# A four-layer graph network on one core: later layers' preparation spread over the steps before they need it, with a new set of planner constants

## The chip, the cores and the metric

The kernel runs on one core of one Trainium2 chip. The metric is the device time of one execution in microseconds (us). A core has a matrix engine (TensorE, PE in the profile, with its weight loads as PEld), a vector engine (VectorE, DVE), a scalar engine (ScalarE, ACT), a general engine (GpSimd, POOL) and a queue that issues DMAs (SyncE, SP). Each works through its own queue in order; semaphores tie them together.

## The reference

There are 32 samples `x` of 512 nodes by 256 features, and one adjacency matrix `adj` of 512 by 512, the same for all samples. Four layers follow each other, each with a layer norm and a relu ahead and a residual behind. Layer 0 is masked multi-head attention with four heads of 64, layer 1 a pair of small graph attention nets with an MLP around them, layer 2 graph attention with four heads of 64, layer 3 the same with eight heads of 32 and a prior made of `adj`:

```python
h = jnp.maximum(_layernorm(x, axis=-1), 0.0)
x = x + _L0_gnn_ref(h, adj, wq, bq, wk, bk, wv, bv, wo, bo)
h = jnp.maximum(_layernorm(x, axis=-1), 0.0)
x = x + _L1_gnn_ref(h, adj, mlp1_w, mlp1_b, mlp2_w, mlp2_b, W_fc, a_fc, W_hand, a_hand)
h = jnp.maximum(_layernorm(x, axis=-1), 0.0)
x = x + _L2_gnn_ref(h, adj, W, a)
h = jnp.maximum(_layernorm(x, axis=-1), 0.0)
x = x + _L3_gnn_ref(h, adj, adj[None], W, a_src, a_dst, beta_tilde, W_out)
```

In layer 3 the attention score of each pair gets `softplus(beta_tilde) * log(prior + 1e-6)` added before a masked softmax. All arithmetic is float32.

## The kernel before

**Preparation.** A first part (lines 400 to 456) loads `adj`, the first sample and the weights of layer 0, transposes `adj`, and makes `mask0T`. What only the later layers need is built by `preparation` as a list of small functions, the pieces: three groups of weight loads (`first_loads`, `second_loads`, `third_loads`, all on SP's queue), `mask_t` (four slices of `mask1T`, VectorE), `output_bias` (the bias of layer 0's output with the value bias folded in: two matmuls and an addition), `fc` (eight) and `hand` (four), which reduce rows of `W_fc` and `W_hand` with the attention vectors of layer 1 on VectorE, `column_sums` (the bias of layer 1's second MLP), `project` (eight) and `scaled` (two), which do the same for layers 2 and 3, `softplus` (beta of layer 3, and the logarithm of the four slices of `mask3T`, on ScalarE), and `mask_3` (four: an exponential on ScalarE and a product with `mask1T` on VectorE).

**The plan.** The work of the 32 samples is not issued as it is written. A `Plan` records every operation as a `Step` (all of them show as L276 in the profile, the line that issues them) with an engine, an assumed duration, what it reads and what it writes. `order` then simulates the engines with these durations and builds one list: at each turn it takes, of all steps that are ready, the one that could start first, and of equals the one that is due first. A step's due time is

```python
step.due = s * self.period - step.tail - step.urgent
```

where `s` is the sample, `period` the constant PERIOD, `tail` the assumed length of the chain from this step to the sample's end, and `urgent` an entry of the table URGENT, looked up by the kind of tile that the step writes and its layer ("p3:3" is the attention weights of layer 3; a negative entry puts them off). STARTS, PACE and LAYERS give the earliest times at which the samples, and the layers in them, may be planned. Buffers are counted too: 62 blocks of 128 x 512 (`tag="block"`) and the 8 banks of PSUM; FILLED = 10 blocks are taken as occupied, by the preparation, until FILLED_TO. Up to four samples are in work at once, and four buffers hold `x`.

**The issue.** `issue` goes through this list and emits the instructions. The pieces of preparation are not in the plan; from step LATE = 30 on, one is emitted at every second step until none is left:

```python
for n, step in enumerate(self.order()):
    if late and n > LATE:
        assert step.layer == 0
        if n % 2:
            late.pop(0)()
    for attribute, op, args, kw in step.calls:
        getattr(getattr(self.nc, attribute), op)(*args, **kw)
```

In the trace the pieces stand under their own lines: L510 to L513 `output_bias`, L519 `column_sums`, L525 `fc`, L531 `hand`, L539 and L540 `project`, L543 and L544 `scaled`, L547 `mask_t`, L551 to L558 `softplus`, L562 and L563 `mask_3`.

**A sample's path.** In layer 0, scores `sc` (TensorE) become `p` (Exp on ScalarE, then times `mask0T` on VectorE), are summed into `total` on VectorE and multiplied with the values into `av`; two heads share a matmul by tiling TensorE's rows or columns. `normalise` sends the sums through DRAM and back as `rc`, `oT` is their product with the copied `av`, and `mm<-woT,oT` closes the layer. An accumulating DMA on GpSimd's queue (`x<-boa`) adds the output bias to `x`; it is the first `dma_start` of that engine in the plan. Layers 2 and 3 (`separable`) make `p3` from broadcast rows `R` in the same way, with `mask1T` and `mask3T`.

Of the kernel before, what the change touches and what calls it, by code (L numbers as in the profile page):

```python
# [22 lines left out]
NT = N // P  # L23
D = 256
KD = D // P
HID = 512
KH = HID // P
# [14 lines left out]

PERIOD = 134.0
STARTS, PACE = (0.0, 0.0, 82.0, 163.0), 113.0
LAYERS = (0.0, 48.0, 0.0, 189.0)

URGENT = {
    "pt:0": 166, "mm:0": 75, "sc:0": 126, "total:0": 49, "pt:1": 25, "mm:1": 40, "nd:1": 9, "p1:1": 126,  # L50
    "total:2": -404, "ue:2": -193, "mm:3": -135, "p3:3": -681, "av:3": -684, "total:3": -608,
}
BLOCKS, KEEP = 62, 2
KEEP_BANKS = 0

LATE = 30

FILLED, FILLED_TO = 10, 120.0
BANKS = ("mm", "av", "sm", "sc", "pt")


# [8 lines left out]
class Plan:  # L70
# [77 lines left out]
    def release(self, sample, layer):  # L148

        first = len(STARTS) - 1  # L150
        return (STARTS[sample] if sample < first else STARTS[first] + (sample - first) * PACE) + LAYERS[layer]

# [112 lines left out]

    def issue(self, tc, late):

        late = list(late)
        with tc.manual_schedule():
            for n, step in enumerate(self.order()):  # L270
                if late and n > LATE:
                    assert step.layer == 0
                    if n % 2:
                        late.pop(0)()
                for attribute, op, args, kw in step.calls:
                    getattr(getattr(self.nc, attribute), op)(*args, **kw)  # L276

# [68 lines left out]
def gnn_stack_kernel(ctx: ExitStack, tc: tile.TileContext, a: dict, out: bass.AP):  # L346
# [18 lines left out]
    def T(ap, rearr, **kw):  # L365
        return ap.rearrange(rearr, **kw)
# [44 lines left out]
    first = ctx.enter_context(tc.tile_pool(name="first", bufs=1))  # L411
# [7 lines left out]
    with prep_stack, tc.manual_schedule():  # L419

        adj = prep.tile([P, NT, N], I32, name="adj", bufs=1)
        av = T(a["adj"], "(t p) j -> p t j", p=P)
# [8 lines left out]
        for name in ("bq", "bk", "bv", "mlp1_b", "mlp2_b"):  # L431
            n = a[name].shape[0]
# [32 lines left out]
    def preparation(block, bank):  # L465

        todo = []
# [94 lines left out]
            nc.scalar.activation(mask3T[:, j, :], mask3T[:, j, :], AF.Exp, scale=beta)  # L562
            nc.vector.tensor_tensor(mask3T[:, j, :], mask3T[:, j, :], mask1T[:, j, :], op=ALU.mult)  # L563

        todo += [first_loads, second_loads, third_loads] + [partial(mask_t, j) for j in range(NT)] + [output_bias]
        todo += [partial(fc, k, c) for k in range(KH) for c in range(2)] + [column_sums]
        todo += [partial(hand, k, c) for k in range(KD) for c in range(2)]
        v2 = [a2[:, None, c * F2 : (c + 1) * F2].to_broadcast([P, H2, F2]) for c in range(2)]
        for w, h, f, vs, vd in ((w2, H2, F2, *v2), (w3, H3, F3, *(T(v, "p (h f) -> p h f", h=H3) for v in (s3, d3)))):
            for k in range(KD):  # L570
                todo += [partial(project, w, k, h, f, vs, w[:, :, :h]), partial(project, w, k, h, f, vd, w[:, :, 3 * h + D :])]
            todo.append(partial(scaled, w, h))
        return todo + [softplus] + [partial(mask_3, j) for j in range(NT)]

    def pipelined(stack):

# [2 lines left out]
        dram = stack.enter_context(tc.tile_pool(name="dram", bufs=6, space=bass.MemoryType.DRAM))  # L579
        q = Plan(nc, PERIOD)  # L580
        def block(name):

            return q.tile(big, [P, N], name, BLOCKS, keep=KEEP, tag="block")
# [433 lines left out]
        for i in range(B):  # L1017
# [9 lines left out]
        q.layer = 3  # L1027
        tests()
        late = preparation(
            lambda n: big.tile([P, N], F32, tag="block", name=n, bufs=BLOCKS),  # L1030
            lambda n: psum.tile([P, N], F32, tag="bank", name=n, bufs=8),
# [424 lines left out]
```

## Time and profile before

| what | us |
|---|---|
| median of 3 runs (3978.35 to 3980.23) | 3978.85 |
| the profiled execution | 3979.58 |
| its span, first to last instruction | 3977.5 |
| TensorE busy | 3888.6 |
| VectorE busy | 3341.5 |
| ScalarE busy | 2807.2 |
| GpSimd busy | 563.8 |

The span is the time that the profile covers; the execution's own time has about 2 us around it. Busy time of TensorE is modelled, since its matmuls are pipelined. A float32 matmul appears as two records: 512 columns take 0.43 us each from start to start. In timelines the number in brackets is the idle time of the engine before a row, with what ended it.

### The profile page before, as it was taken

How to read it: one execution, taken by the hardware profiler on the slowest of the kernel's cores; microseconds unless marked ns; L12 is line 12 of the kernel's file. 1: busy time of each engine (PE TensorE's matmuls, PEld its weight loads, DVE VectorE, ACT ScalarE, POOL GpSimd, SP SyncE). 2: the span in 40 equal slices, each digit the busy share in tenths (PEclk: the TensorE clock that was granted, in tenths of full speed). 3: DMA queues.
4: the chain of work that ended last, by engine and by line, in shares of the span. 5: the costliest groups of instructions: out<-in, count | busy, mean ns of one | idle time of the engine just before them, and what ended most of it. 6: DMA issues, size and time to landing. Idle time of an engine off the chain costs nothing.

```text
span 3977.5 us, 52568 instructions
## 1 busy us (share of the span) xinstructions
PE 3888.6 (98%) x17144; PEld 2146.2 (54%) x17144; DVE 3341.5 (84%) x7049; ACT 2807.2 (71%) x5968; POOL 563.8 (14%) x530
## 2 busy tenths in 40 slices
PE   7999999999999999999999999999999999999986
PEld 3655555565555555555555555555555555555542
DVE  6389988888988888988888988888988889888886
ACT  4467667776777766777766777666777767677665
POOL 0001111101111111111101111011111011111010
PEclk8999999999999999999999999999999999999998
DMA  3013333313233233333223333132333233333231
GB/s 92 17 49 76 75 84 83 80 55 89 59 89 91 62 74 73 72 89 83 65 65 81 73 88 86 51 89 57 83 92 77 58 76 75 84 83 77 64 74 51
DMA packets 217617, 292.58 MB, mean 74 GB/s; under 512 B 49915, under 2 KB 103422, under 8 KB 217334
## 3 DMA queue, kind: packets, MB, share of 16 engines
q0 software_dynamic: 68864, 111.18, 16.1%
q1 hardware_dynamic: 148196, 177.69, 14.3%
q8 instruction: 138, 2.26, 0.2%
q14 instruction: 145, 1.19, 0.1%
q10 hardware_dynamic: 274, 0.26, 0.0%
HBM read 158.79 MB, written 19.10 MB: 45 GB/s over the span
## 4 chain that ended last, share of the span: by engine, by line
PE 70%; DVE 17%; DMA 5%; ACT 4%; issue 2%; POOL 2%; SPq 1%; DVEq 0%; ACTq 0%; POOLq 0%
PE mm L276 33%; PE av L276 23%; PE sc L276 5%; PE pt L276 5%; DVE p L276 5%; DVE total L276 5%; DMA R<-rd 4%; PE sm L276 3%; POOL rs L276 2%; DVE o L276 1%; ACT p L276 1%; DVE x L276 1%; DVE ue L276 1%; DVE stats L276 1%; DVE y L276 1%
## 5 line engine op out<-in xcount | busy, mean ns | idle before, releaser
L276 ACT ACTIVATE p<-R,e 128x512 f32<-128x512 f32 x1536 | 987.7, 724 | 53.0 <-DMA R<-rd 52.9
L276 PE MATMUL av<-p,v 128*128 128x512 f32 (+1 forms) x2560 | 933.8, 598 | 13.0 <-ACT p L276 10.7
L276 DVE SCALAR_TENSOR_TENSOR p<-p,e,mask3T 128x512 f32<-128x512 f32 x1024 | 718.8, 749 | 16.9 <-ACT p L276 16.9
L276 POOL TENSOR_TENSOR rs<-ve,mhalf 128x4 f32<-128x4 f32 x128 | 206.5, 1613 | 2755.6 <-DVE ve L276 2202.6
L276 PEld LDWEIGHTS av<-p,v 128*128 128x128 f32 (+1 forms) x2560 | 347.6, 169 | 458.0 <-issue 367.3
L276 DVE TENSOR_TENSOR total<-total,p 128x512 f32<-128x512 f32 x872 | 573.2, 689 | 0.5
L276 PE MATMUL av<-p,vs 128*32 128x512 f32 (+1 forms) x3072 | 494.9, 597 | 5.3 <-DVE p L276 5.0
L276 PE MATMUL mm<-W_fc,o 128*128 128x256 f32 (+1 forms) x2048 | 469.0, 380 | 2.5 <-ACT o L276 2.3
L276 PEld LDWEIGHTS mm<-W_fc,o 128*128 128x128 f32 x2048 | 382.3, 190 | 86.5 <-issue 29.4
L276 POOL DMA_DIRECT2D p<-p x360 | 317.3, 1014 | 579.5 <-PE av L276 161.9
L276 DVE SCALAR_TENSOR_TENSOR p<-p,e,mask1T 128x512 f32<-128x512 f32 x512 | 347.9, 750 | 41.4 <-ACT p L276 40.7
L276 ACT ACTIVATE h<-x,ms,rs 128x256 f32<-128x256 f32 x512 | 282.8, 629 | 128.5 <-DVE ms L276 128.4
L276 DVE TENSOR_TENSOR p<-p,mask0T 128x512 f32<-128x512 f32 x512 | 329.3, 690 | 20.0 <-ACT p L276 20.0
L276 PEld LDWEIGHTS av<-p,vs 128*32 128x32 f32 (+1 forms) x3072 | 136.5, 118 | 334.8 <-issue 234.3
L276 DVE TENSOR_TENSOR total<-p,p 128x512 f32<-128x512 f32 x436 | 289.2, 688 | 0.0
L276 ACT ACTIVATE p<-sc 128x512 f32<-128x512 f32 x512 | 254.4, 684 | 6.1 <-PE sc L276 6.1
L276 PE MATMUL mm<-w,hT 128*128 128x272 f32 (+1 forms) x1024 | 254.0, 394 | 1.1 <-ACT hT L276 1.0
L276 PE MATMUL mm<-hT,mlp_w 128*128 128x512 f32 x512 | 237.3, 595 | 0.6 <-ACT hT L276 0.6
L276 PE MATMUL mm<-o,mlp_w 128*128 128x512 f32 x512 | 234.2, 595 | 0.3
L276 PE MATMUL sc<-qT,kT 64*128 64x512 f32 x1024 | 228.4, 596 | 0.0
L276 PEld LDWEIGHTS mm<-w,hT 128*128 128x128 f32 x1024 | 191.3, 192 | 61.5 <-issue 14.3
L276 ACT COPY v<-mm 128x512 f32<-128x512 f32 (+2 forms) x384 | 166.1, 470 | 43.7 <-PE mm L276 40.7
(182 smaller groups left out, 5321.1 us busy)
## 6 DMA issues: line engine op xcount, KB each, us to landing
R<-rd SPq DMA_DIRECT2D x384, 256.0 KB
p<-p POOLq DMA_DIRECT2D x360, 256.0 KB, 5.4
x<-in_x_dram SPq DMA_DIRECT2D x32, 512.0 KB
x<-boa POOLq DMA_DIRECT2D x32, 512.0 KB, 5.6
rc<-s SPq DMA_DIRECT2D x128, 128.0 KB
out_dram<-x SPq DMA_DIRECT2D x32, 512.0 KB
rc<-s SPq DMA_DIRECT2D x248, 64.0 KB
s<-sums SPq DMA_DIRECT2D x94, 8.0 KB
```

The lines of the kernel that those rows point to most:

```text
L276: getattr(getattr(self.nc, attribute), op)(*args, **kw)
```

## The change

Three things are changed. The constants of the plan (PERIOD, STARTS, PACE, LAYERS, URGENT, FILLED_TO) take other values. The list of pieces carries with each piece the layer that it has to precede: 0 for the loads and `output_bias`, 1 for `fc`, `column_sums`, `hand` and `mask_t`, 2 for `project`, `scaled`, `softplus` and `mask_3`. And `issue` distributes the pieces of each group evenly, by step number: those of group 0 between step 30 and the first accumulating DMA of GpSimd, those of group 1 from there to the first step of layer 1, those of group 2 from there to the first step of layer 2. `mask_t`, which came before `output_bias`, now comes after `hand`; else the order in the list is kept.

```diff
-PERIOD = 134.0
-STARTS, PACE = (0.0, 0.0, 82.0, 163.0), 113.0
-LAYERS = (0.0, 48.0, 0.0, 189.0)
+PERIOD = 179.0
+STARTS, PACE = (0.0, 0.0, 38.0, 159.0), 85.0
+LAYERS = (0.0, 4.0, 2.0, 98.0)
 
 URGENT = {
-    "pt:0": 166, "mm:0": 75, "sc:0": 126, "total:0": 49, "pt:1": 25, "mm:1": 40, "nd:1": 9, "p1:1": 126,
-    "total:2": -404, "ue:2": -193, "mm:3": -135, "p3:3": -681, "av:3": -684, "total:3": -608,
+    "pt:0": 192, "mm:0": 49, "total:0": 70, "av:0": 68, "mm:1": 25, "total:1": -78, "rs1:1": 42, "av:1": -7,
+    "p2:1": 104, "p3:2": -95, "total:2": -542, "ue:2": -396, "mv:3": -121, "mm:3": -158, "p3:3": -723,
+    "av:3": -527, "total:3": -695,
 }
...
-FILLED, FILLED_TO = 10, 120.0
+FILLED, FILLED_TO = 10, 190.0
...
-        late = list(late)
+        steps, at = self.order(), {}
+        begin = LATE
+        for layer in range(3):
+
+            pieces = [f for need, f in late if need == layer]
+            first = next(n for n, step in enumerate(steps) if step.layer > layer - 1 and n > begin) if layer else next(n for n, step in enumerate(steps) if step.calls[0][1] == "dma_start" and step.engine == "POOL")
+            for i, f in enumerate(pieces):
+                at.setdefault(begin + (first - begin) * i // len(pieces), []).append(f)
+            begin = first
         with tc.manual_schedule():
-            for n, step in enumerate(self.order()):
-                if late and n > LATE:
-                    assert step.layer == 0
-                    if n % 2:
-                        late.pop(0)()
+            for n, step in enumerate(steps):
+                for f in at.get(n, ()):
+                    f()
                 for attribute, op, args, kw in step.calls:
                     getattr(getattr(self.nc, attribute), op)(*args, **kw)
...
-        todo += [first_loads, second_loads, third_loads] + [partial(mask_t, j) for j in range(NT)] + [output_bias]
-        todo += [partial(fc, k, c) for k in range(KH) for c in range(2)] + [column_sums]
-        todo += [partial(hand, k, c) for k in range(KD) for c in range(2)]
+        todo += [(0, f) for f in (first_loads, second_loads, third_loads, output_bias)]
+        todo += [(1, partial(fc, k, c)) for k in range(KH) for c in range(2)]
+        todo += [(1, column_sums)] + [(1, partial(hand, k, c)) for k in range(KD) for c in range(2)]
+        todo += [(1, partial(mask_t, j)) for j in range(NT)]
...
-                todo += [partial(project, w, k, h, f, vs, w[:, :, :h]), partial(project, w, k, h, f, vd, w[:, :, 3 * h + D :])]
-            todo.append(partial(scaled, w, h))
-        return todo + [softplus] + [partial(mask_3, j) for j in range(NT)]
+                todo += [(2, partial(project, w, k, h, f, vec, dst)) for vec, dst in ((vs, w[:, :, :h]), (vd, w[:, :, 3 * h + D :]))]
+            todo.append((2, partial(scaled, w, h)))
+        return todo + [(2, softplus)] + [(2, partial(mask_3, j)) for j in range(NT)]
```

## The prediction

> **What bounds the kernel now.** I read the page first, then busy time by windows, then the timelines of TensorE and ScalarE where a window is not full, and last the end of the chain of waits.
>
> ```profile
> span 3977.5 us, 52568 instructions
> ...
> PE 3888.6 (98%) x17144; PEld 2146.2 (54%) x17144; DVE 3341.5 (84%) x7049; ACT 2807.2 (71%) x5968; POOL 563.8 (14%) x530
> ...
> PEclk8999999999999999999999999999999999999998
> ```
>
> TensorE is idle for 3977.5 - 3888.6 = 88.9 us in all. The windows say where: of the first 400 us it is busy 370.3 (idle 29.7), from 400 to 3800 it is busy 3384.8 of 3400 (idle 15.2), from 3800 to the end 133.6 of 177.5 (idle 43.9). So the whole change can win only at the start, at the end, or by making the packed middle itself denser.
>
> ```profile
> 40.00:60.00 20.00, 9.35 (x33) 3.26 (x30) 13.28 (x34) 13.55 (x25) 0.00 (x0) 0.66 0.00 0
> 60.00:80.00 20.00, 20.00 (x77) 9.04 (x76) 12.90 (x22) 8.27 (x15) 0.00 (x0) 1.00 0.01 2
> 80.00:100.00 20.00, 15.35 (x58) 7.89 (x58) 18.20 (x33) 6.25 (x13) 0.00 (x0) 0.83 0.08 27
> ...
> 643.60:883.90 240.30, 239.28 (x1057) 132.16 (x1056) 207.59 (x437) 173.84 (x373) 36.96 (x34) 1.00 0.32 76
> ...
> 3769.70:3977.40 207.70, 163.86 (x843) 83.29 (x841) 153.39 (x318) 121.09 (x258) 16.44 (x16) 0.90 0.25 68
> ```
>
> The columns are the stretch, its length, busy time (and count) of TensorE, its weight loads, VectorE, ScalarE, GpSimd, then TensorE's granted clock, DMA share and GB/s. Two holes stand at 40 to 60 and 80 to 100 us. The fourth line is one steady round of two samples (outputs leave at 643.6 and 883.9): 240.3 us with TensorE busy 239.3. The last line is what is left after the 29th sample is stored. The two early holes, in TensorE's timeline:
>
> ```profile
> 55.11 7.01 PE L276 MATMUL av<-p,v 128*64 128x512 f32 x16 [10.65 <-ACT p L276]
> ...
> 92.51 6.27 PE L276 MATMUL mm<-woT,oT 128*128 128x256 f32 x16 [4.65 <-DVE oT L276]
> ```
>
> The first hole is 10.65 us and the 16 records after it take 7.01 us; the same group takes 3.65 at 73.56. The second is 4.65 us, and its group takes 6.27 where the steady timeline gives about 0.215 per record, 3.44. So the holes cost 10.65 + 3.36 and 4.65 + 2.83, together 21.5 us. ScalarE's timeline shows what the first one waits for:
>
> ```profile
> 48.89 0.20 ACT L554 ACTIVATE ab<-ab 128x1 f32<-128x1 f32 x1 [6.39 <-DVE ab L553]
> 49.11 1.28 ACT L555 ACT_TABLE_LOAD   x1
> 50.40 0.29 ACT L555 ACTIVATE ab<-ab 128x1 f32<-128x1 f32 x1
> 50.60 2.54 ACT L557 ACTIVATE mask3T<-mask3T,eps 128x512 f32<-128x512 f32 x4
> 53.16 1.28 ACT L276 ACT_TABLE_LOAD   x1
> 54.46 0.60 ACT L276 ACTIVATE p<-sc 128x512 f32<-128x512 f32 x1
> ```
>
> Eight exponentials end at 42.5; the ninth stands behind the softplus piece, which waits 6.39 us for VectorE (busy with other pieces) and then takes 5.57 us with its two table loads. All eight banks hold scores by then, so TensorE's next product has no bank until 54.46 plus 0.6. VectorE ends the other side of it: the end of the chain is
>
> ```profile
> 3881.35 19.88 DVE p L276 x30
> ...
> 3936.22 16.56 DVE p L276 x25
> ```
>
> two runs of layer 3's attention weights on VectorE, with latencies of DMA and normalisation between them.
>
> **What the Trainium skill says.** "TensorE: Matmul & The Clock Gate", section "What's actually happening": TensorE falls to half clock after an idle window of about 3.4 us and comes back after as much sustained work. The trace agrees: the holes of 10.65 and 4.65 us are followed by records at twice their length. "ScalarE: Activation LUTs", "What ACT_TABLE_LOAD costs": about 1.28 us for the load and more for a drain; here the load is 1.28 and the next activation starts 0.01 to 0.02 us later, so I use 1.28. "TensorEngine Tiling (Array Packing)", "Key Properties": a change of tiling mode drains TensorE. I grouped TensorE's records from 643.6 to 3529.3 us into runs of one mode: 217 runs, where a run of column-tiled products lasts a median 0.43 us longer than its records at full rate, a full-size run 0.28. All that lies above the full rate is 108.7 us for 24 samples, 4.5 per sample, of which about 0.5 is idle.
>
> **The change, part by part.**
>
> *Fewer pieces in the first layer 0.* From the timeline, VectorE's pieces by start-to-start: fc 8 x 0.73 = 5.9, hand 4 x 0.46 = 1.9, mask1T 4 x 0.40 = 1.6, sums 0.2: 9.6 us, still ahead of layer 1. project 8 x 0.90 = 7.2, scaled and softplus 0.9, mask_3 4 x 0.60 = 2.4: 10.5 us of VectorE and 0.2 + 1.28 + 0.29 + 2.54 + 1.28 + 4 x 0.62 = 8.1 us of ScalarE leave it for the stretch in which sample 0 is in layer 1. Before, 12.4 us of pieces run on VectorE between 36.6 and 60. With softplus gone, the ninth exponential can follow the eighth at about 43 and a bank is free before TensorE asks for it. Then VectorE decides: 28 products and sums of 0.60 for one sample, 16.8 us from 41.9, plus the third or so of the 9.6 us that falls there. TensorE has the second sample's projections ready meanwhile (10.5 us, they run at 62.04 before). I take 11 of the 14.0 us of the first hole; between 0 and 14. The second hole has VectorE working without a break from 78.9, with sample 1's weights ahead of sample 0's normalisation. Sample 2 may now be planned from 38 instead of 82, which gives TensorE something to do, but VectorE more. I take half, 3.5 of 7.5; between -4 and 7.5. Sum -14.5.
>
> *The pieces at their new place.* Before, TensorE is full from 120 to 280 us while VectorE has 8 to 16 us of each 20 busy and ScalarE 6 to 17: 10.5 and 8.1 us spread there are covered. The one lump is softplus, 5.6 us on ScalarE in one piece, with the copies that free TensorE's banks queued behind it; if TensorE runs out of banks in that time it stands, and its clock may fall too. Between 0 and 9; I take +2. All DMAs of the weights now come as three groups between step 30 and the first accumulating DMA, not within six steps; the same count on SP's queue, before the first `rc` transfers there; the first fc uses them at 30.0 us before, layer 1 itself from 104. Later by 10 us they cost nothing; the cover gone would be a wait at the first fc, in order on VectorE. The matmuls of the two bias pieces are the same number.
>
> *Returned later.* From 345 to 373 us the chain is VectorE (busy 27.07 of 28) and the first four samples pile up. Who arrives earlier waits there. TensorE idles only 0.6 us in it, so I take +1.5; between 0 and 10.
>
> *The planner's numbers: the end.* How far an operation of layer 3 is put behind, in sample periods, is its entry over PERIOD: p3:3 681/134 = 5.1 before, 723/179 = 4.0 after; av:3 5.1 against 2.9; total:3 4.5 against 3.9; layer 2's total 3.0 both times. Layer 3 is left over less at the end, where its weights are the chain for 36 us. The end costs 43.9 idle and, by the clock records, about 11 of half clock. Between +10 and -25; I take -8.
>
> *The planner's numbers: the middle.* No view tells how the new order comes out. It cannot win more than the 4.5 us per sample named above; lost could be as much. With the idle time alone as measure I take -0.18 per sample, 28 samples, -5; between -60 and +60.
>
> **Sum** against the profiled execution, 3979.58 (span 3977.5 and 2.1 around it): -14.5 + 2 + 1.5 - 8 - 5 = -24, so 3955.6. The median of the runs is 0.7 lower: 3955.
>
> **The rivals.**
>
> *A denser middle.* The new priorities keep the column-tiled products together, one run less per sample (0.43 + 0.28, with some idle 1.0): -28, the end wins 20, the start 14: about 3917. For it: 4.5 us per sample are there. Against: TensorE is already idle for 0.4% of the middle.
>
> *Given back.* The holes close, but the time returns at 345 to 373 and at the end, where the last samples' latencies (11.00 us before one L3 product, 5.21 before the next) don't care when it began. Also here: the pieces are spread by step number, not by time, so they could bunch and keep a hole. About 3972.
>
> *A looser middle, slower.* Ordering by the larger PERIOD and the nearer av:3 breaks column-tiled runs apart or lets TensorE wait on VectorE, busy 86% of a round. Its place is the round of 240.3 us; its price 0.71 us per sample for one further switch to and fro, 28 times, 20 us. From +0.85 us per sample (24/28) it eats everything; two more switches (+40, without the -5) give 3979 - 19 + 40 = 4000. For it: seven deferrals are changed at once and nothing in the profile binds them. Against: relative to PERIOD most of them stay close.
>
> **How the numbers follow.** What a measurement of this kernel tells from no change is about 0.2%, 8 us. My forecast 0.45 (3925 to 3970), denser 0.13, given back 0.16 (0.10 of it faster than 3971, 0.06 within), looser 0.26. So faster 0.68, same 0.06, slower 0.26. Time 3955. The range must reach into both outer cases: 3908 to 4000 leaves out about half of the looser middle and a third of the denser one.
>
> **What would show it.** ScalarE: no table load between 40 and 60 us, two between about 90 and 200. TensorE: 40 to 60 us busy over 16 at a clock over 0.9; idle of the first 400 us about 15 to 18, not 29.7. A round of two samples within 239 to 241 us; if it is 242 or more, the middle was the mistake. After the 29th output less than 200 us, against 207.7. A new ScalarE wait of TensorE at the softplus piece over 5 us would show that its new place is not covered.

## The result, and the profile after

The changed kernel takes 3964.52 us (median of 6 runs, 3960.09 to 3966.82), the kernel before 3978.6 in the same comparison: ratio 0.9965, 95% interval 0.9953 to 0.9978. That is 14 us less, of the 24 that were forecast. The profiled execution has a span of 3962.9 us, 14.6 below that of before.

The page of the changed kernel:

```profile
span 3962.9 us, 52558 instructions
...
PE 3890.9 (98%) x17144; PEld 2149.1 (54%) x17144; DVE 3344.2 (84%) x7049; ACT 2805.9 (71%) x5968; POOL 566.4 (14%) x530
...
PEclk8999999999999999999999999999999999999998
```

Each engine's busy time is within 3 us of that of before; TensorE's idle time falls from 88.9 to 72.0 us. Its busy time by windows (columns as in the prediction):

```profile
40.00:60.00 20.00, 20.00 (x78) 9.12 (x74) 17.23 (x34) 8.72 (x17) 0.00 (x0) 1.00 0.00 0
60.00:80.00 20.00, 16.86 (x75) 6.94 (x75) 15.35 (x34) 8.94 (x18) 0.00 (x0) 0.91 0.09 28
80.00:100.00 20.00, 19.26 (x69) 9.51 (x68) 13.38 (x40) 9.82 (x18) 2.03 (x2) 0.92 0.07 23
...
140.00:160.00 20.00, 16.18 (x53) 9.25 (x51) 7.77 (x27) 14.87 (x27) 1.01 (x1) 0.91 0.00 0
...
634.30:874.60 240.30, 239.49 (x1058) 132.52 (x1057) 207.98 (x438) 174.37 (x374) 36.98 (x34) 1.00 0.32 76
3759.10:3962.90 203.80, 168.32 (x843) 83.89 (x841) 153.93 (x318) 121.41 (x258) 15.10 (x16) 0.91 0.25 69
```

The hole at 40 to 60 us is gone: 20.00 of 20 busy at full clock, against 9.35 at 0.66. The second is still there, a little earlier and smaller. A third is new, at 140 to 160. A round of two samples takes 240.3 us as before, and after the 29th output 203.8 us pass instead of 207.7. TensorE's timeline shows what the two remaining holes wait for:

```profile
79.51 5.00 PE L283 MATMUL av<-p,v 128*64 128x512 f32 x12 [3.14 <-DVE p L283]
...
154.76 1.12 PE L283 MATMUL pt<-ident,h 128*128 128x128 f32 x4 [2.19 <-ACT h L283]
...
160.04 0.65 PE L283 MATMUL pt<-ident,ew 128*128 128x128 f32 x4 [1.58 <-DVE nd L283]
```

and ScalarE's timeline shows the softplus piece in its new place, with a normalised `h` and the four copies of `v` behind it:

```profile
149.97 0.19 ACT L561 ACTIVATE ab<-ab 128x1 f32<-128x1 f32 x1
150.18 1.28 ACT L562 ACT_TABLE_LOAD   x1
151.47 0.29 ACT L562 ACTIVATE ab<-ab 128x1 f32<-128x1 f32 x1
151.67 2.54 ACT L564 ACTIVATE mask3T<-mask3T,eps 128x512 f32<-128x512 f32 x4
154.12 0.58 ACT L283 ACTIVATE h<-x,ms,rs 128x256 f32<-128x256 f32 x1
154.61 1.16 ACT L283 COPY v<-mm 128x258 f32<-128x258 f32 x4
```

At the end of the chain of waits the last stretch of layer 3's weights on VectorE is not shorter: two runs follow each other closely, 7.58 and 11.35 us, where one of 16.56 stood. But the run of 19.88 before it has given way to two of 8.65 and 3.41 and to matmuls. After the 29th output the runs of over 3 us come to 41.1 us before and 31.0 after:

```profile
3862.37 8.65 DVE p L283 x13
...
3871.65 3.41 DVE p L283 x5
...
3919.04 7.58 DVE p L283 x12
...
3927.00 11.35 DVE p L283 x17
3938.35 7.04 DVE rc L283 x3
```

To compare many kernels I use one measure, worked out from the trace: the *loss* of a stretch is its length less the time that TensorE's records starting in it take at full rate (0.429 us for a record of 512 columns, 0.2155 for 256, 0.109 for 128, divided by the number of tiles side by side). It holds idle time, half clock and changes of tiling mode (of the shape of the tiles into which TensorE is divided) alike. The records come to 3723.5 us in every kernel here, so the losses add up to the difference in span. Rows e1 to e12 are the experiments below.

| loss, us | 0-40 | 40-60 | 60-120 | 120-200 | 200-400 | 400-3700 | to the end | median us |
|---|---|---|---|---|---|---|---|---|
| before | 20.1 | 13.6 | 12.5 | 0.2 | 5.4 | 124.0 | 78.2 | 3978.6 |
| change | 18.7 | 0.9 | 11.4 | 8.0 | 5.5 | 123.2 | 71.7 | 3964.5 |
| change, again (e10) | 21.7 | 0.7 | 11.1 | 10.1 | 6.7 | 119.7 | 72.9 | 3964.5 |
| e1 spread only | 19.6 | 1.4 | 14.3 | 5.9 | 5.3 | 126.0 | 77.9 | 3970.3 |
| e2 constants only | 19.7 | 13.8 | 8.4 | 0.1 | 6.9 | 117.1 | 73.1 | 3965.4 |
| e3 softplus held | 20.8 | 6.3 | 12.2 | 4.9 | 5.4 | 124.7 | 77.0 | 3976.7 |
| e4 softplus early | 21.3 | 0.7 | 11.1 | 5.1 | 6.4 | 118.5 | 72.3 | 3960.7 |
| e5 old priorities | 21.7 | 1.7 | 14.3 | 6.6 | 5.1 | 124.5 | 75.5 | 3970.9 |
| e6 old releases | 20.0 | 1.4 | 17.6 | 9.4 | 24.4 | 159.5 | 72.9 | 4029.7 |
| e8 old starts | 22.6 | 1.5 | 17.8 | 9.8 | 24.1 | 154.3 | 74.0 | 4028.2 |
| e9 old layers | 19.6 | 0.7 | 11.7 | 7.9 | 6.4 | 119.3 | 71.6 | 3962.6 |
| e7 fill early | 20.4 | 1.1 | 8.3 | 4.9 | 5.9 | 118.1 | 71.4 | 3959.7 |
| e7 again (e11) | 22.1 | 1.1 | 8.6 | 4.7 | 5.7 | 120.0 | 72.7 | 3955.6 |
| e12 layer 1 clear | 22.5 | 0.7 | 7.6 | 1.8 | 9.4 | 117.2 | 72.9 | 3957.4 |

One profile stands behind each row of losses. The two of the change differ by 3 us in the first 40 us and 3.5 in the middle, so differences of that size in one column are not read alone. The first column above all depends on how the execution began: the change gave 18.7 and 21.7, e7 20.4 and 22.1. The last section tells the two forms apart.

### The profile page after: what moved, and what is told of

The parts are those of the page before. It is cut to its first block, busy times and chain, and to the rows that moved or that the text cites. A ratio compares the mean times of both kernels' runs of the same rounds, so it can differ in the third digit from the quotient of the medians.

```text
span 3962.9 us, 52558 instructions
## 1 busy us (share of the span) xinstructions
PE 3890.9 (98%) x17144; PEld 2149.1 (54%) x17144; DVE 3344.2 (84%) x7049; ACT 2805.9 (71%) x5968; POOL 566.4 (14%) x530
## 3 DMA queue, kind: packets, MB, share of 16 engines
q1 hardware_dynamic: 148196, 177.69, 14.3%
## 4 chain that ended last, share of the span: by engine, by line
PE 69%; DVE 17%; DMA 5%; ACT 4%; issue 2%; POOL 2%; SPq 1%; DVEq 0%; ACTq 0%; POOLq 0%
PE mm L283 33%; PE av L283 22%; PE sc L283 5%; PE pt L283 5%; DVE total L283 5%; DVE p L283 5%; DMA R<-rd 4%; PE sm L283 3%; ACT p L283 2%; POOL rs L283 2%; DVE o L283 1%; DVE ue L283 1%; DVE stats L283 1%; DVE x L283 1%; DVE y L283 1%
## 5 line engine op out<-in xcount | busy, mean ns | idle before, releaser
L283 PE MATMUL av<-p,vs 128*32 128x512 f32 (+1 forms) x3072 | 504.5, 598 | 5.6 <-DVE p L283 5.4
L283 ACT COPY rc<-pt 128x512 f32<-128x512 f32 x64 | 37.4, 585 | 246.8 <-PE pt L283 246.7
```

## The experiments

**Which half of the change.** The first experiment takes the new `issue` and list of pieces with all the old constants; the second takes the new constants with the old `issue` and list.

```diff
 e1, against the change
-PERIOD = 179.0
-STARTS, PACE = (0.0, 0.0, 38.0, 159.0), 85.0
-LAYERS = (0.0, 4.0, 2.0, 98.0)
+PERIOD = 134.0
+STARTS, PACE = (0.0, 0.0, 82.0, 163.0), 113.0
+LAYERS = (0.0, 48.0, 0.0, 189.0)
 (URGENT and FILLED_TO as before, too)
```

> The pieces are spread as in the change, the planner's constants stay as before. Theory A (the softplus piece in front of the exponentials of the first layer 0 made the first hole; spreading it closes the hole whatever the constants): against full rate TensorE loses at most 6 us between 20 and 60 us where it lost 17.8 before, a new loss of 3 to 7 us stands where softplus lands in layer 1, the end after the 29th output stays at about 207.7; time about 3970, ratio 0.997 to 0.999. Theory B (the constants made the gain): the first 200 us still lose 44 to 48 us, ratio 1.000.

Measured: 3970.32, ratio 0.9983 (0.9976 to 0.9991). Between 20 and 60 us 5.0 lost, 5.9 at 120 to 200, the last stretch 208.3. That is theory A.

> The planner's constants of the change with the pieces where they were, one at every second step from step 30 on. Theory A: a hole of 8 to 12 us comes back between 40 and 60 us, the first 200 us lose 44 us or more, but the stretch after the 29th output is as short as after the change (about 204); time about 3973, ratio 0.998 to 0.9995. Theory B: time about 3965, ratio 0.9965, the first 200 us lose 39 us or less.

Measured: 3965.39, ratio 0.9971 (0.9960 to 0.9983). TensorE's timeline has the first hole as it was:

```profile
54.68 7.01 PE L277 MATMUL av<-p,v 128*64 128x512 f32 x16 [10.66 <-ACT p L277]
```

So the hole is tied to the pieces, as A says, but the time is B's: the constants alone win 12 us with the hole still open. They win at the second hole (8.4 against 12.5), in the middle and at the end. The first 200 us lose 42.0, between the two forecasts.

Each half wins (7 and 12) and both together 14: the gains do not add. Put on top of the new constants, spreading the pieces closes 12.9 us of the first hole and loses 3.0 at 60 to 120 and 7.9 at 120 to 200. What is left is within the noise: the ratios 0.9971 and 0.9965 have overlapping intervals. So of the 14 us of the change, the half that closes the first hole adds next to nothing to the other half.

**Who made the first hole.** The kernel before, with softplus and mask_3 alone moved to layer 1 (the lines that emit the held pieces are left out here):

```diff
-        late = list(late)
+        late, held, at, steps = list(late[:-5]), late[-5:], {}, self.order()
+        begin, first = (next(n for n, step in enumerate(steps) if step.layer > layer) for layer in (0, 1))
+        for i, f in enumerate(held):
+            at.setdefault(begin + (first - begin) * (10 + i) // 15, []).append(f)
...
```

> The kernel before with one thing moved: softplus and the four mask_3 wait until sample 0 is in layer 1; all other pieces and the constants stay. Theory A (softplus on ScalarE alone made the first hole): the loss between 20 and 60 us falls from 17.8 to 7 or less, and 3 to 7 us come back near 150. Rival C (VectorE, busy with all the pieces, made it): the loss between 20 and 60 us stays at 12 or more.

Measured: the loss from 20 to 60 falls from 17.8 to 10.9, between the two. The wait itself is clear, in TensorE's timeline of this kernel:

```profile
47.71 1.07 PE L281 MATMUL av<-p,v 128*64 128x512 f32 x2 [0.78 <-DVE p L281]
50.55 3.91 PE L281 MATMUL av<-p,v 128*64 128x512 f32 x8 [1.76 <-DVE p L281]
```

10.65 us behind ScalarE are gone, and ScalarE runs its 16 exponentials in one go; 2.5 us behind VectorE, busy with the other pieces, come out from under it. Both causes are real, softplus the larger: 7.3 us of the 12.7 that the change wins at 40 to 60 us. VectorE has a part in the 10.65 us too: softplus itself waited 6.39 us for it before, as the prediction's lines show. The time, 3976.73, ratio 0.9994 (0.9986 to 1.0003), says little: 4.7 us come back at 120 to 200.

**What the new place costs.** The changed kernel with mask_t and softplus ahead of the first query copy. The number in front of a piece is the group that it belongs to; the new group -1 is emitted there:

```diff
+        early = next(
+            n for n, step in enumerate(steps)
+            if step.engine == "ACT" and self.kinds.get(step.calls[0][2][0].tensor.name) == "qT"
+        )
+        at.setdefault(early, []).extend(f for need, f in late if need < 0)
...
-        todo += [(1, partial(mask_t, j)) for j in range(NT)]
+        todo += [(-1, partial(mask_t, j)) for j in range(NT)] + [(-1, softplus)]
...
-        return todo + [(2, softplus)] + [(2, partial(mask_3, j)) for j in range(NT)]
+        return todo + [(2, partial(mask_3, j)) for j in range(NT)]
```

> The changed kernel with mask_t and softplus moved ahead of the first query copy, to about 20 us, where VectorE idles 11 us and ScalarE 5. Theory A (what the new place costs is softplus on ScalarE, 6.5 us of TensorE between 140 and 160): that loss falls under 1.5, at most 2 are added at 25 to 40 us, time about 3960, ratio to before 0.995 to 0.996. Rival D (the loss at 140 to 160 comes from the new order of the steps themselves): it stays over 4, time 3964 or more.

Measured: 3960.68, ratio 0.9956 (0.9943 to 0.9970). The loss at 140 to 160 falls from 6.5 to 2.2, which lies between the two forecasts, but from 160 to 180 it grows from 0.6 to 2.7; over 120 to 200 it is 5.1, against 8.0 and 10.1 in the two profiles of the change. So softplus is 3 to 5 us of it (mask_t moved with it, but stood at 79 to 89 us in the change, ahead of this stretch). The last experiment below takes up the rest.

**Which constants.** PERIOD and URGENT set back (e5), and the mirror of it (e6):

```diff
 e5
-PERIOD = 179.0
+PERIOD = 134.0
 (URGENT as before, too)
 e6
-STARTS, PACE = (0.0, 0.0, 38.0, 159.0), 85.0
-LAYERS = (0.0, 4.0, 2.0, 98.0)
+STARTS, PACE = (0.0, 0.0, 82.0, 163.0), 113.0
+LAYERS = (0.0, 48.0, 0.0, 189.0)
-FILLED, FILLED_TO = 10, 190.0
+FILLED, FILLED_TO = 10, 120.0
```

> The changed kernel with PERIOD and URGENT set back to what they were; STARTS, PACE, LAYERS and FILLED_TO keep the new values. Theory E (the shorter end comes from the priorities): the stretch after the 29th output is back at 207 to 208 us and what is lost after 3700 us at 77 to 78; time about 3970. Rival F (it comes from the earlier releases of layers and samples): the stretch stays at 204 to 205, time 3965.

Measured: 3970.92, ratio 0.9983 (0.9977 to 0.9990); last stretch 207.0 us. That is theory E, though the loss after 3700 us, 75.5, came back less far than the 77 to 78 that it forecast.

> The mirror of the one before: the changed kernel with STARTS, PACE, LAYERS and FILLED_TO set back, PERIOD and URGENT new. Theory E: the stretch after the 29th output is 203 to 205 us, time 3963 to 3967. Rival F: 207 to 208, time 3970.

Measured: last stretch 201.4 us, as short as E says and shorter, and a time that neither had: 4029.68, ratio 1.0132 (1.0117 to 1.0148). The end depends on the priorities; but the same priorities with the old releases cost 65 us elsewhere, 19 of it from 200 to 400 and 36 from 400 to 3700. Two more kernels tell which release it is.

```diff
 e8
-STARTS, PACE = (0.0, 0.0, 38.0, 159.0), 85.0
+STARTS, PACE = (0.0, 0.0, 82.0, 163.0), 113.0
 e9
-LAYERS = (0.0, 4.0, 2.0, 98.0)
+LAYERS = (0.0, 48.0, 0.0, 189.0)
```

> The changed kernel with STARTS and PACE alone set back; LAYERS, FILLED_TO, PERIOD and URGENT new. Theory I (the 65 us that old releases cost come from when the third and fourth sample start: they set how the samples of a pair stand to each other): the outputs up to the tenth leave in an irregular order instead of 80 and 160 us apart, time over 4010. Rival J (it is the release of the layers): even gaps of 80 and 160 us from the second output on, time 3963 to 3970.

> The changed kernel with LAYERS alone set back; STARTS, PACE, FILLED_TO, PERIOD and URGENT new. Theory I: gaps of 80 and 160 us, time 3963 to 3972. Rival J: irregular gaps up to the tenth output, time over 4010.

Measured: 4028.18 (ratio 1.0121, 1.0091 to 1.0150) and 3962.62 (0.9957, 0.9938 to 0.9977). Theory I; which of STARTS and PACE it is was not set apart, and LAYERS and FILLED_TO, set back as well in e6, make no difference to speak of. The outputs of e8, from the timeline of SP's queue:

```profile
412.33 0.41 SPq L283 DMA_DIRECT2D out_dram<-x  x1
524.98 0.40 SPq L283 DMA_DIRECT2D out_dram<-x  x1
678.82 0.40 SPq L283 DMA_DIRECT2D out_dram<-x  x1
728.84 0.40 SPq L283 DMA_DIRECT2D out_dram<-x  x1
896.00 0.40 SPq L283 DMA_DIRECT2D out_dram<-x  x1
1023.99 0.40 SPq L283 DMA_DIRECT2D out_dram<-x  x1
```

The gaps are 113, 154, 50, 167, 128 us and settle to 80 and 160 only after the ninth output, where the change has them from the first gap on (80.6, 159.7, 80.3). Once settled, e8's rounds are as long as the others' (240 us). The third sample's load is issued at 101.8 us there and at 25.7 in the change. Why this start leads to that order was not followed further.

**The middle.** The change once more, for a second profile:

> The changed kernel once more, for a second profile of its middle. Four other kernels with the new PERIOD and URGENT lose 117 to 119 us against full rate between 400 and 3700 us, four with the old ones 124 to 126, the changed kernel's one profile 123.2. Theory K (the new priorities do win about 5 us in the middle and that profile was a poor draw): 117 to 120 here. Rival L (the middle differs from one execution to the next by that much, or the changed kernel's own middle is slower): 122 or more.

Measured: 119.7, and 3964.47 us. Over all kernels with regular rounds the middle loses 117 to 123 with the new priorities (eight profiles, mean 119.1) and 124.0 to 126.0 with the old (four, mean 124.8). K holds in the mean, about -5.7 us; that the first profile was an outlier of a few us is likely, not shown. A count in TensorE's records goes with it: if column tiles of 64 and of 32 are taken as two modes, there are 421 runs of one mode from the third to the 27th output in all four profiles with the old priorities and 397 in all eight with the new. Those are 24 fewer switches between the two widths for 24 samples. A run that ends at such a switch lasts a median 0.14 to 0.15 us longer than its records at full rate, so by estimate about 4 of the 5.7 us could be this; no run sets it apart.

**A better version.** Besides softplus and mask_t, fc, hand and column_sums go ahead of output_bias (group -2), into the 11 us in which VectorE is idle there:

```diff
+        bias = next(n for n in sorted(at) if n > early)
+        at[bias] = [f for need, f in late if need < -1] + at[bias]
...
-        todo += [(1, partial(fc, k, c)) for k in range(KH) for c in range(2)]
-        todo += [(1, column_sums)] + [(1, partial(hand, k, c)) for k in range(KD) for c in range(2)]
+        todo += [(-2, partial(fc, k, c)) for k in range(KH) for c in range(2)]
+        todo += [(-2, column_sums)] + [(-2, partial(hand, k, c)) for k in range(KD) for c in range(2)]
```

> The changed kernel with mask_t and softplus at about 20 us as in the run before, and fc, hand and column_sums as well ahead of output_bias, so that VectorE does them in its idle stretch from 20 to 31 us. Theory G (the second hole, 60 to 100 us, is VectorE's backlog and the pieces are a part of it): the loss between 60 and 100 us falls from 11.4 to 6 or less, that between 140 and 160 under 2.5, time about 3955, ratio to before 0.9945. Rival H (the backlog is the attention's own products and sums): the loss between 60 and 100 stays at 9 or more and the time at 3960; if the loads have not landed by 22, VectorE waits for them and a new hole appears at 36 to 45.

> The version with the pieces filled into VectorE's idle stretch at 20 to 31 us, beside the changed kernel on the same chip. Theory G: its median is 3 to 7 us below the changed kernel's, the first 200 us lose about 35 us against 39. Rival H: within 2 us of it.

Measured: 3959.70 (ratio 0.9957, 0.9944 to 0.9971), then beside the change on one chip 3955.63 (0.9948, 0.9935 to 0.9962) against 3964.47 (0.9968, 0.9955 to 0.9980). It is faster than both kernels, by 9 us than the change in that comparison (more than G's 3 to 7), by 5 in medians of different ones. In the first 200 us it loses 36.5 in the second profile, against 43.6 in that of the change beside it. The second hole goes from 11.4 to 8.3 and 8.6, between the forecasts and nearer to H: VectorE's pieces were about 3 us of it. That the rest is the attention's own work is what H says, not shown. The loss at 140 to 160 stays at 3.9 and 3.5, over G's 2.5. Against e4, with softplus early alone, the time is not clearly better: 0.9957 and 0.9948 against 0.9956. VectorE's timeline of this version shows that the loads were there in time, except the one of beta:

```profile
20.52 1.43 DVE L562 TENSOR_SCALAR mask1T<-mask3T 128x512 bf16<-128x512 f32 x4
...
24.76 0.15 DVE L567 TENSOR_SCALAR ab<-ab 128x1 f32<-128x1 f32 x1 [2.81 <-DMA ab<-in_beta_dram]
...
27.11 0.69 DVE L540 CUSTOM_DVE_ANT_0 prf<-W_fc,afc 128x512 f32<-128x512 f32 x1
```

Last, no piece at all while sample 0 is in layer 1 (against e7):

```diff
-        for layer in range(3):
+        for layer in range(4):
...
-                todo += [(2, partial(project, w, k, h, f, vec, dst)) for vec, dst in (...)]
-            todo.append((2, partial(scaled, w, h)))
+                todo += [(-2 if h == H2 else 3, partial(project, w, k, h, f, vec, dst)) for vec, dst in (...)]
+            todo.append((-2 if h == H2 else 3, partial(scaled, w, h)))
-        return todo + [(2, partial(mask_3, j)) for j in range(NT)]
+        return todo + [(3, partial(mask_3, j)) for j in range(NT)]
```

> The version with the filled idle stretch, and now no piece at all while sample 0 is in layer 1: project and scaled of layer 2 join the early ones, those of layer 3 and mask_3 go between the first step of layer 2 and the first of layer 3. Between 140 and 180 us TensorE still loses about 5 us with softplus gone from there. Theory M (the other pieces there make it): under 1.5 now; time 3951 to 3956, unless the moved pieces cost it again between 200 and 400. Theory N (TensorE, with the first hole closed, runs ahead of the latencies of sample 0's layer 1, pieces or none): 4 or more remains, time 3955 to 3960.

Measured: 3957.39, ratio 0.9950 (0.9937 to 0.9964). Its windows:

```profile
140.00:160.00 20.00, 20.00 (x69) 11.56 (x68) 10.11 (x26) 12.43 (x24) 1.01 (x1) 1.00 0.00 0
160.00:180.00 20.00, 19.75 (x88) 14.14 (x87) 9.81 (x25) 9.73 (x22) 2.27 (x2) 1.00 0.10 16
```

From 140 to 180 us 0.9 is lost: theory M. But from 200 to 400 it is 9.4 against 5.9. The pieces put off until then stand at 173 to 245 us, and the added loss at 220 to 260 (4.7 against 1.2), where VectorE is busy 18.26 and 16.43 of 20 us. The time is that of the version before within the spread.

## Why the prediction was right

The direction and the range held, and the mechanism of the largest term: the first hole stood behind softplus and closed when that was moved. The size was 24 for 14. By the terms of its sum, read from the first profile of the change:

- *The first hole*, taken at -11: 17.8 to 3.7 from 20 to 60 us, so -14.1, all of it. That softplus on ScalarE was the cause is shown by e3 for the wait of 10.65 us; e1 and e2 show that the constants have next to no part in it.
- *The second hole*, taken at -3.5: -1.1 (12.5 to 11.4 from 60 to 120). The reason given, that an earlier third sample gives TensorE something to do, is not borne out by itself: with spread pieces and old constants the loss is 14.3, with the new releases but old priorities also 14.3 (e5), with both new 11 to 12. Under the new priorities alone it holds: with the old starts they lose 17.8 there (e8), with the new 11.4. That VectorE stands behind the hole was read rightly: it is what TensorE waits 3.14 us for at 79.51.
- *The pieces at their new place*, taken at +2, in a range of 0 to 9: +7.8. This is the term that was most mis-sized. Softplus made 3 to 5 us of it and the other pieces about 3 (e4, e7, e12: 5.1, 4.9, 1.8); with no piece there 1.8 is left. The prediction took all but the lump of softplus as covered, because VectorE and ScalarE had room in the windows of the kernel before; e12 shows that the other pieces (project, scaled and mask_3) cost about 3 us there all the same. (Its reading of the windows was also too low for 220 to 240 us, where VectorE is busy 19.08 of 20, not 16 at most.) One could think that the cover was real before, when TensorE was behind and had ready work in store, and went with the hole. That is not shown: in e3 TensorE has lost 39.3 us by 120 us, 46.2 before and 31.0 in the change, and 4.9 us come back at 120 to 200 there already.
- *Returned later*, taken at +1.5: +0.1. VectorE's full stretch at 345 to 373 us gave nothing back, in e12 neither.
- *The end*, taken at -8: -6.5, and about -4.7 between the means of all kernels with new and old priorities (72.5 and 77.2). That it comes from the priorities is shown by e5 and e6.
- *The middle*, taken at -5: -0.8 in that profile, about -5.7 in the mean. The argument for it was a mere allowance, by idle time, and that did not change: TensorE is idle 15.2 us from 400 to 3800 before and after. That the mean comes near is luck. The prediction's own count, with column tiles of both widths as one mode, is 217 runs before and after. Counted by width there are 24 switches fewer, one per sample as in the rival of the denser middle, but at about 0.15 us each, not 0.7 to 1.0.

The measured terms add up to -14.6, the difference of the two spans. But they are not independent, as the sum takes them: next to the constants alone, the pieces' new place gives in one stretch what it takes in the next. So the forecast of "faster" would have come true by the constants even if the holes had stayed.

Of the signs that the prediction named, the table loads, the full window at 40 to 60 us and the round of 240.3 us came as written. TensorE's idle time in the first 400 us is 21.3, not 15 to 18, and after the 29th output 203.8 us pass, not under 200. The sign set for a bad new place, a wait for ScalarE of over 5 us, did not show: the wait is 2.19 us. The place costs 7.8 us without it, in several short waits and 3.4 us at half clock after that one.

The looser middle as written, one or two more mode changes per sample, did not occur. A slowing larger than its 20 to 40 us is near, though, through a thing that the prediction did not name: the priorities hold only with start times that suit them (65 us, e6 and e8).

## What to carry to other kernels

A piece that is outside the plan costs what stands behind it on its in-order queue: ask which engine is idle, before the work that needs it, and put it there, as the version with VectorE's idle 11 us does. Cover cannot be read from busy shares alone: softplus cost 3 to 5 us where every window had room, because an `h` that TensorE waited for stood behind it. Test the halves of a change apart and together: a half that closes a hole of 13 us can be worth next to nothing beside the other. And constants that order a plan are one set: start times that cost nothing under one set of priorities (e1, e5: 3970.3 and 3970.9) cost 65 us under another.

## What was not expected of the hardware

In the first profile of the change TensorE ran at half clock from 62.6 to 66.0 us though it shows no idle time just before: from 59.57 it had run 16 records of one column (column_sums) and eight tiled ones. In the second profile of the same kernel this half clock is missing. Short idle times can be enough: those of 3.14 us before 79.51 and 2.19 us before 154.76 were each followed by 3.4 us at half clock (79.6 to 83.1 and 154.7 to 158.1), less than the idle window that the prediction reckons with.

The start has two forms. In eight of the fourteen profiles the first record of full clock comes at 8.0 to 9.7 us, and TensorE's 24 one-column products at about 8 to 9 us take 2.8 to 3.2 us; the first 40 us lose 18.7 to 20.8. In the other six it comes at 26.7 to 29.3 us, the 24 products take 5.28, and the first 40 us lose 21.3 to 22.6. The first statistics of the layer norm on VectorE wait for these products: in the change its first wait ends at 16.7 us in one profile (2.83) and at 20.0 in the other (5.28). The trace has no clock record ahead of the first one, but the length of the products that follow shows half clock in both: the first two records of 512 columns (at 20.18 and 23.48 us) take 2.07 us in either profile, and two of them 1.02 once full clock is recorded. Which form an execution gets was not controlled. It is likely a part of the 3 to 10 us by which the times of one kernel differ; that is not shown.
